# A causal mask added by matrix products instead of by VectorE and GpSimd, and a shorter routing chain, in a Perceiver-like layer

## The chip, the cores and the metric

The kernel runs on one core of a Trainium2 chip. The metric is the device time of one execution in microseconds; several executions are timed and the median counts. Engines are named as in the profile: PE (TensorE, the matrix engine), PEld (its weight loads), DVE (VectorE), ACT (ScalarE), POOL (GpSimd) and SP (SyncE, which here only issues DMAs).

## The reference

Two batches of 512 tokens of width 512 pass three blocks, each behind a layer norm and with a residual addition.

```python
x = x + cross_attention(norm(x), ctx, mask)   # 16 heads of 32, 8192 keys per batch
x = x + self_attention(norm(x))               # 16 heads of 32, causal, 512 keys
x = x + mixture(norm(x))                      # 16 experts, top 2, capacity 64 per batch

# self-attention: amplitudes and phases
q_amp = softplus(x @ Wq_amp.T); q_phi = pi * tanh(x @ Wq_phi.T)     # and so for k
q_amp = q_amp / sqrt(mean(q_amp**2) + eps)
scores = (q_amp cos(q_phi)) . (k_amp cos(k_phi)) + (q_amp sin(q_phi)) . (k_amp sin(k_phi))
scores = where(tril, scores / sqrt(32) * exp(log_scale), -inf)
out = softmax(scores) @ v @ Wo.T

# mixture: a token's place among those of its expert
g = softmax(x @ w_router); p, ei = top_k(g, 2)      # first choices of all tokens, then second ones
pos = cumsum(one_hot(ei)) - 1                       # tokens beyond the capacity are dropped
y = sum_k p_k * expert[ei_k](x)                     # (silu(x Wg) * (x Wf)) Wp
```

## The kernel before

The layer is one straight program; its order on each engine is the order in which it is written. Matrix products are float32 where nothing else is said, and the trace shows each as two passes over the moving columns.

**Cross-attention** (0 to about 2520 us) runs over 64 steps, 16 chunks of 1024 keys by 4 groups of 4 heads. Work of the self-attention of batch 0 (norm, phases, amplitudes) is filled into its last steps, and `sa_tables` makes the constants of the self-attention early in it, on POOL, DVE and ACT: `s_minus`, and `causal`, a 128x128 tile that holds 0 where the key is not later than the query and -2^100 elsewhere.

**Self-attention** (`self_attention`, to about 2834 us) works on groups of 4 heads, `g` from 0 to 3 for each batch. The four heads lie on four bands of 32 partitions, so that four products with 32 contraction rows run side by side on PE, each into a PSUM bank of its own. All banks come from one ring of eight (`bank()`); a product waits until the bank's last reader is done. Scores are made twice:

- `score_max` makes them with queries on the partitions, in three parts per group (`x` 0: queries 384 to 511 against 512 keys; 1: 256 to 383 against 384; 2: the two others, against 256 and 128). DVE adds `causal` to the square on the diagonal (L1181, L1188) and takes each row's maximum, `scm` (L1182, L1189, L1190). `split` then cuts the maxima into three bfloat16 parts, and `max_rows` turns them into `rows` with 16 small bfloat16 products (L194) and a copy on ACT (L1207).
- `score_exp` makes them again with keys on the partitions (`product`, L1155), in three parts of key tiles 0, 1 and 2 with 3. A bfloat16 product with `s_minus` and `rows` subtracts the maxima (L1224, four row groups of 3 rows), ACT takes the exponential into `e` (L1227), and POOL sets the squares' upper part of `e` to zero by a selection over 4 heads at once (L1229):

```python
for own in ([e[:, :, 0:P]] if x < 2 else [e[:, :, 0:P], e[:, :, 2 * P : 3 * P]]):
    nc.gpsimd.affine_select(out=own, in_=own, pattern=[[0, 4], [1, P]],
        compare_op=ALU.is_ge, fill=0.0, base=0, channel_multiplier=-1)
```

`attend` writes the order: per group the three exponentials, between them the maxima of four parts further on (`AHEAD`), then the weighted values (L1242) and the row sums (L1283) of two key tiles, `max_rows` of the next group, and the other two tiles. A chain on DVE ends the group (transpose, reciprocal, transpose, product: `srec`, `few`, `wide`, `soT`, L1303 to L1308) and frees the two banks of values and sums. `first_maxima` makes the first four parts of the maxima ahead of `attend`, between other products. In gaps named by group and part (`fill`) stands work of the other batch: for batch 0 the amplitudes and values of batch 1, for batch 1 the routing of batch 0.

**Routing** (`route`, once per batch) returns a list of pieces: norm statistics of four token tiles, `scale` (root and one Newton step), the four tiles normalised and stored to the DRAM tensor `normed`, four turns on PE into `mxnT`, then `router` (16 products, L764, and the row maximum, the differences and their exponential), `probabilities`, `top(0)` and `top(1)` (one-hot of first and second choice, `oh`), `counted` (running sums over the tiles on DVE, `so_far`), `ranked` (three products, L806, L809, L810, give each token's place; `hit` and `whose`) and `numbered` (16 PE instructions, L835, give each expert's list of tokens, `token`). For batch 0 the pieces lie in the gaps of batch 1's attention. For batch 1 they run after it, in a plain line: four times the output projection of a tile (`output`, L194, then L1316 on DVE) with its statistics and one expert's loads on SP, then all other pieces. Then POOL issues 16 gathers (`fetch`, `gx`, L852), which wait for `token` and the stores, and the **experts** start (L873, L890) and end at about 2963 us. The results are gathered back and added.

Of the kernel before, what the change touches and what calls it, by code (L numbers as in the profile page):

```python
# [20 lines left out]
P = 128  # L21
# [21 lines left out]
def perceiver_kernel(ctx: ExitStack, tc: tile.TileContext, a, out: bass.AP):  # L43
# [45 lines left out]
    lnp = ctx.enter_context(tc.tile_pool(name="ln", bufs=2))  # L89

    def norm_pieces(b, keep=None, aside=False):
# [52 lines left out]
        tiles = Tiles()  # L144
        pieces = [lambda i=i: stats(i) for i in range(TB)]
# [584 lines left out]
    def route(b, ps, pstag, ps1):  # L730
# [24 lines left out]
        pr, mx, sr = tile("pr", [P, TB, E]), tile("mx", [P, TB]), tile("sr", [P, TB])  # L755
        oh = tile("oh", [P, 2, TB, E])
        pk[b] = tile("pk", [P, 2, TB])

        def router():
            bank = ps1.tile([P, TB, P], F32, tag="j", name="pl")  # L760
            pl = bank[:, :, :E]
            for i in range(TB):
                for c in range(ND):
                    nc.tensor.matmul(  # L764
                        pl[:, i, :],
                        mxnT[:, c, i * P : (i + 1) * P],
                        mo.wr[:, c, :],
                        start=(c == 0),
                        stop=(c == ND - 1),
                    )  # L770
            nc.vector.tensor_reduce(mx, pl, AX.X, ALU.max)
            nc.vector.tensor_tensor(pr, pl, over_e(mx), ALU.subtract)
            nc.scalar.activation(pr, pr, AF.Exp)

        def probabilities():
            nc.vector.tensor_reduce(sr, pr, AX.X, ALU.add)
            nc.vector.reciprocal(sr, sr)
            nc.vector.tensor_tensor(pr, pr, over_e(sr), ALU.mult)

        def top(k):  # L780

            nc.vector.tensor_reduce(pk[b][:, k, :], pr, AX.X, ALU.max)
            eq, fm = tile(f"eq_{k}", [P, TB, E]), tile(f"fm_{k}", [P, TB])
            nc.vector.tensor_tensor(eq, pr, over_e(pk[b][:, k, :]), ALU.is_equal)
            nc.vector.tensor_tensor(eq, eq, over_t(mo.falling), ALU.mult)
            nc.vector.tensor_reduce(fm, eq, AX.X, ALU.max)
            nc.vector.tensor_tensor(oh[:, k], eq, over_e(fm), ALU.is_equal)
            if k == 0:
                nc.vector.scalar_tensor_tensor(pr, oh[:, k], -4.0, pr, ALU.mult, ALU.add)


        so_far = tile("sofar", [P, 2, TB, E])

        def counted():
            nc.vector.tensor_copy(so_far[:, :, 0, :], oh[:, :, 0, :])
            for i in range(1, TB):
                nc.vector.tensor_tensor(so_far[:, :, i, :], so_far[:, :, i - 1, :], oh[:, :, i, :], ALU.add)
# [3 lines left out]

        def ranked():

            bank = ps1.tile([P, S], F32, tag="j", name="pp")
            pp = bank[:, : 2 * TB * E].rearrange("p (k t e) -> p k t e", k=2, t=TB)
            nc.tensor.matmul(  # L806
                bank[:, : 2 * TB * E], mo.before, oh.rearrange("p k t e -> p (k t e)"), start=True, stop=False
            )
            nc.tensor.matmul(pp[:, :, 1:, :], ones, so_far[:, :, : TB - 1, :], start=False, stop=False)  # L809
            nc.tensor.matmul(  # L810
                pp[:, 1], ones, so_far[:, 0, TB - 1 : TB, :].to_broadcast([P, TB, E]), start=False, stop=True
            )
            for k in range(2):
                t, f = tile(f"rank_{k}", [P, TB, E]), tile(f"from_{k}", [P, TB, E])
                nc.vector.tensor_tensor(f, oh[:, k], over_t(mo.first_slot), ALU.mult)
# [676 lines left out]
```

## Time and profile before

| | before |
|---|---|
| median of 3 executions | 3010.15 us |
| lowest and highest | 3001.26 and 3014.18 us |
| the profiled execution | 3000.01 us, span 2998.3 us |
| mean granted clock of PE | 0.988 |
| busy share of PE, DVE, ACT, POOL | 97%, 67%, 47%, 73% |

The profile is of one execution. Its span runs from the first to the last instruction, and some 1.7 us lie around it. A line of the profile's groups reads: line of the kernel, engine, operation, what it writes and reads, shapes, count; then busy time and mean duration of one in ns; then the idle time of the engine just before and what ended it. PE's products are pipelined: the duration of one includes its way through the array, so what a product costs in a row is read from the starts. PE is busy for most of the span, so a step on another engine counts only where PE waits for it, and a step on PE counts nearly always.

### The profile page before, as it was taken

The page shows a single profiled execution, that of the slowest core. Times are in us where ns is not written, and L with a number is a line of the kernel's source. Part 1 is how long each engine was busy: PE and PEld are TensorE (multiplying, and loading weights), DVE is VectorE, ACT ScalarE, POOL GpSimd, SP SyncE. Part 2 cuts the span into 40 slices and gives each one's busy share as a digit, 9 for nine tenths or more (in the row PEclk, how much of TensorE's full clock was granted, in tenths as well). Part 3 has the DMA queues.
Part 4 walks back from the last instruction along what each step waited for, and adds up shares of the span by engine and source line. Part 5 has one row for each costly group of instructions (what it writes and reads, how often), then busy time and mean ns, then how long its engine had stood idle before and what let it go on. Part 6 is the DMA issues. An engine that isn't in the chain of part 4 may idle for free.

```text
span 2998.3 us, 64624 instructions
## 1 busy us (share of the span) xinstructions
PE 2899.7 (97%) x27911; PEld 1112.5 (37%) x27911; DVE 1997.8 (67%) x3397; ACT 1394.9 (47%) x2609; POOL 2175.4 (73%) x873
## 2 busy tenths in 40 slices
PE   7999999999999999999999999999999999999875
PEld 2333333333333333333333333333333332344564
DVE  6566777777777777766777776677777666668522
ACT  1355555555555555445555555555555436563210
POOL 1598888888888888978888888888888772011022
PEclk9999999999999999999999999999999999999987
DMA  3000000000000000000000000000000002011384
GB/s 124 1 24 1 24 2 24 2 24 6 20 8 18 16 9 23 2 1 24 1 24 2 24 1 24 1 24 1 24 2 1 29 30 71 1 43 45 105 259 128
DMA packets 48141, 89.65 MB, mean 30 GB/s; under 512 B 4720, under 2 KB 23152, under 8 KB 47856
## 3 DMA queue, kind: packets, MB, share of 16 engines
q1 hardware_dynamic: 40832, 70.31, 7.1%
q0 software_dynamic: 2752, 8.39, 0.9%
q10 hardware_dynamic: 4272, 6.83, 0.7%
q8 instruction: 218, 3.57, 0.5%
q14 instruction: 67, 0.55, 0.1%
HBM read 77.13 MB, written 8.39 MB: 29 GB/s over the span
## 4 chain that ended last, share of the span: by engine, by line
PE 92%; DVE 4%; ACT 1%; issue 1%; DMA 1%; POOL 1%; ACTq 0%; POOLq 0%; DVEq 0%
PE s L194 31%; PE s L423 18%; PE s L488 16%; PE s L436 15%; PE s L455 4%; PE s L1155 2%; PE ph L873 2%; PE s L515 2%; PE po L890 1%; DVE cm L445 1%; PE s L1242 1%; DVE acc L523 1%; PE s L1283 1%; PE s L167 0%; POOL r L918 0%
## 5 line engine op out<-in xcount | busy, mean ns | idle before, releaser
L654 POOL TENSOR_TENSOR es<-es,e 128x2048 f32<-128x2048 f32 x374 | 1700.7, 4547 | 54.9 <-ACT e L457 38.0
L457 ACT ACTIVATE e<-s 128x512 f32<-128x512 f32 x2048 | 1057.3, 603 | 1110.9 <-PE s L455 1110.9
L445 DVE TENSOR_REDUCE cm<-s 128x1 f32<-128x512 f32 x2048 | 1271.1, 683 | 330.8 <-PE s L423 330.7
L423 PE MATMUL s<-k,qT 32*128 32x512 f32 x4096 | 587.2, 640 | 3.4 <-DVE cm L445 1.9
L436 PE MATMUL s<-qT,k 32*128 32x512 f32 x4096 | 554.7, 593 | 3.1 <-ACT e L457 2.3
L488 PE MATMUL s<-e,v 128*32 128x512 f32 x4096 | 495.2, 600 | 1.1 <-DVE cm L445 0.8
L654 POOL TENSOR_TENSOR es<-e 128x2048 f32<-128x2048 f32 x63 | 286.2, 4542 | 243.0 <-ACT e L457 243.0
L194 PE MATMUL s<-wkv,ctx 128*32 128x512 f32 x3072 | 365.4, 596 | 0.4
L194 PE MATMUL s<-ctx,wkv 128*32 128x512 f32 x3072 | 355.9, 596 | 0.5
L436 PEld LDWEIGHTS s<-qT,k 32*128 32x128 f32 x4096 | 282.3, 184 | 185.1 <-issue 106.4
L503 DVE TENSOR_TENSOR acc<-acc,s 128x512 f32<-128x512 f32 (+1 forms) x359 | 207.8, 604 | 138.5 <-PE s L488 137.9
L423 PEld LDWEIGHTS s<-k,qT 32*128 32x128 f32 x4096 | 161.6, 182 | 330.7 <-issue 258.2
L488 PEld LDWEIGHTS s<-e,v 128*32 128x32 f32 x4096 | 107.4, 109 | 320.0 <-DVE cm L445 160.9
L455 PE MATMUL s<-rows,mb 4*128 4x512 bf16 x2048 | 218.0, 376 | 0.0
L399 DVE SCALAR_TENSOR_TENSOR k<-s,kf,m 128x512 f32<-128x512 f32 x128 | 96.1, 751 | 171.7 <-PE s L194 171.7
L194 PEld LDWEIGHTS s<-ctx,wkv 128*32 128x32 f32 x3072 | 87.1, 109 | 235.2 <-issue 154.3
L194 PEld LDWEIGHTS s<-wkv,ctx 128*32 128x32 f32 x3072 | 86.9, 109 | 214.3 <-issue 125.9
L414 ACT COPY v<-s 128x512 f32<-128x512 f32 x128 | 74.9, 585 | 98.1 <-PE s L194 77.3
L511 DVE TENSOR_TENSOR acc<-acc,s 128x1024 f32<-128x1024 f32 x56 | 68.4, 1221 | 71.1 <-ACT s L510 71.1
L455 PEld LDWEIGHTS <-mb 4*128 4x128 bf16 x2048 | 68.5, 93 | 105.5 <-issue 99.4
L1197 POOL TENSOR_TENSOR rest<-scm,parts 128x16 f32<-128x16 f32 x8 | 2.0, 254 | 139.9 <-DVE parts L1195 139.9
L1229 POOL TENSOR_SCALAR_AFFINE_SELECT e<-e 128x512 f32<-128x512 f32 x32 | 22.1, 703 | 105.9 <-ACT e L1227 105.9
(259 smaller groups left out, 1917.3 us busy)
## 6 DMA issues: line engine op xcount, KB each, us to landing
ctx<-in_ctxT_dram SPq DMA_DIRECT2D x45, 512.0 KB
wg<-in_L_ffn_w_gate_dram SPq DMA_DIRECT2D x16, 512.0 KB
wf<-in_L_ffn_w_fc_dram SPq DMA_DIRECT2D x16, 512.0 KB
wp<-in_L_ffn_w_proj_dram SPq DMA_DIRECT2D x16, 512.0 KB
results<-res ACTq DMA_DIRECT2D x32, 128.0 KB
m<-in_mask_BxS_bf_dram SPq DMA_DIRECT2D x16, 128.0 KB
w_wq_phiT<-in_wq_phiT_dram SPq DMA_DIRECT2D x2, 1024.0 KB
w_wq_ampT<-in_wq_ampT_dram SPq DMA_DIRECT2D x2, 1024.0 KB
```

The source lines that it names most:

```text
L194: nc.tensor.matmul(out[q], lhsT[:, q], rhs, start=start, stop=stop)
L399: nc.vector.scalar_tensor_tensor(k[:, keys], bank, kf[:, g, b : b + 1], mask_tiles[i][:, keys], ALU.subtract, ALU.mult)
L414: nc.scalar.copy(v[:, kt % (NKT // 2), :], bank)
L423: nc.tensor.matmul(s, qT(chunks[i][0], g, r, slice(qt * P, (qt + 1) * P)), k_tiles[n][r, hf * S : (hf + 1) * S], start=True, stop=True,)
L436: nc.tensor.matmul(s, k_tiles[n][r, keys], qT(chunks[i][0], g, r, slice(0, S)), start=True, stop=False)
L445: nc.vector.tensor_reduce(cms[g][chunks[i][1] % 2][:, qt, j : j + 1, hf], ss[j], AX.X, ALU.max)
L455: nc.tensor.matmul(ss[j], bias_tiles[i][r4, keys], rows[r4, :], start=False, stop=True)
L457: nc.scalar.activation(e[:, j, :], ss[j], AF.Exp)
L488: nc.tensor.matmul(av[j * HD : (j + 1) * HD, :], v_tiles[i][kt // (NKT // 2)][:, kt % (NKT // 2), h * HD : (h + 1) * HD], e[:, j, :], star ...
L503: nc.vector.tensor_tensor(dst, dst, src, ALU.add)
L511: nc.vector.tensor_tensor(acc[g], acc[g], pa.unsqueeze(1).to_broadcast([P, 2, S]), ALU.mult)
L654: nc.gpsimd.tensor_tensor(es, first if kt == 1 else es, e, ALU.add)
```

## The change

Two things are changed.

The **mask** of both kinds of scores becomes part of the scores' accumulation in PSUM. `sa_tables` no longer makes `causal`, but two bfloat16 tables on POOL: `which`, four stacked 32x32 unit matrices in the middle of zeros, and `bounds`, which holds 0, a triangle, and -2^100. A window of `which` as weights moves 32 rows of the mask to one quarter of the 128 output rows, so four products per head, 16 per square, add the whole mask. Additions on DVE and selections on POOL go.

The **routing** finds the first choice from the differences to the maximum (equal to 0) before the exponential is there, counts with products alone (24 PE instructions for 6, no running sums on DVE), makes `hit` in two halves, and moves the probabilities behind `numbered`. For batch 1 `route` returns `in_line`: the first three tiles are normalised (on ACT) under the last output product and turned ahead of the fourth; the last turn's copy is shared by ACT and DVE; and a one-element sigmoid follows the routing.

```diff
-                        nc.vector.tensor_tensor(s[:, qt * P : w], s[:, qt * P : w], sa.causal, ALU.add)
+                    masked(ss, slice(qt * P, w), sa.later)          # score_max, x < 2
...
+                    masked(ss, slice(P, 2 * P), sa.later)           # score_max, x == 2, two squares
+                    masked(ss, slice(2 * P, 3 * P), sa.later)
...
                     product(ss, b, g, 1, slice(kt * P, (kt + 1) * P), 0, slice(kt * P, S), at)
+                    masked(ss, slice(w, w + P), sa.sooner, False)   # score_exp, every key tile
...
-                for own in ([e[:, :, 0:P]] if x < 2 else [e[:, :, 0:P], e[:, :, 2 * P : 3 * P]]):
-                    nc.gpsimd.affine_select(...)
...
+            def masked(ss, at, mask, last=True):
+                for n in range(4):
+                    for j in range(4):
+                        r, c = slice(j * HD, (j + 1) * HD), slice((3 - n) * HD, (7 - n) * HD)
+                        nc.tensor.matmul(ss[j][:, at], sa.which[r, c], mask[r, c], start=False, stop=(last and n == 3))
...
+        def top_first():
+            nc.vector.tensor_reduce(mx[:, 0], pl, AX.X, ALU.max)
+            nc.vector.tensor_tensor(d, pl, over_e(mx[:, 0]), ALU.subtract)
+            nc.scalar.activation(pr, d, AF.Exp)
+            nc.vector.scalar_tensor_tensor(eq, d, 0.0, over_t(mo.falling), ALU.is_equal, ALU.mult)
+            first(0, eq)                       # two more steps on DVE: oh[:, 0]
...
+        def counted(k):
+            nc.tensor.matmul(pp[:, k], mo.before, oh[:, k], start=(k == 0), stop=False)
+            for i in range(1, TB):
+                nc.tensor.matmul(pp[:, k, i:], ones, oh[:, k, : TB - i], start=False, stop=(i == TB - 1))
+            if k == 0:
+                for i in range(TB):
+                    nc.tensor.matmul(pp[:, 1], ones, oh[:, 0, i : i + 1, :].to_broadcast([P, TB, E]), ...)
...
-        return pieces + [router, probabilities, lambda: top(0), lambda: top(1), counted, ranked, numbered]
+        found = [top_first, lambda: (counted(0), top_second()), lambda: counted(1), ranked, numbered, probabilities]
+        def in_line(output, between):
+            last = TB - 1
+            for i in range(TB):
+                output(i)
+                tiles.stats(i)
+                between(i)                     # loads of an expert
+                if i == last - 1:
+                    tiles.scale_of(0, last)
+                    for j in range(last):
+                        tiles.scaled(j)        # normalised on ACT
+                        stored(j)
+            turn(ps, pstag, tiles[0], mxnT[:, :, :P], nc.scalar.copy)
+            tiles.scale_of(last, TB)
+            for j in range(1, last):
+                turned(j)
+            tiles.normed(last)
+            stored(last)
+            turn(ps, pstag, tiles[last], mxnT[:, :, last * P :], halves)   # ACT and DVE, half each
+            router()
+            for f in found:
+                f()
+            nc.scalar.activation(tile("warm", [P, 1]), eps, AF.Sigmoid)
+        return in_line if split else pieces + [router, *found]
```

The pieces of batch 0 keep their number and their gaps; what stands in the last three gaps is now `top_first` with `counted(0)` and `top_second`, then `counted(1)` with `ranked`, then `numbered` with `probabilities`.

## The prediction

> **What bounds the kernel now.** I read the page's busy shares first, then the stages of the second half as windows, then what PE waited for in the self-attention, then groups and single starts there, and last the chain at the end.
>
> ```profile
> PE 2899.7 (97%) x27911; PEld 1112.5 (37%) x27911; DVE 1997.8 (67%) x3397; ACT 1394.9 (47%) x2609; POOL 2175.4 (73%) x873
> ```
>
> PE is the bound as a whole. The 73% of POOL belong to the cross-attention, which the change doesn't touch. The stages that it does touch (columns: stretch, its length, then busy us and count for PE, PEld, DVE, ACT, POOL, then clock, DMA share, GB/s):
>
> ```profile
> 2606.00:2711.00 105.00, 98.59 (x1152) 41.25 (x1148) 72.08 (x145) 59.57 (x97) 15.54 (x33) 1.00 0.11 37
> 2711.00:2737.00 26.00, 26.00 (x289) 10.97 (x287) 21.79 (x48) 6.19 (x7) 1.85 (x4) 1.00 0.25 82
> 2737.00:2822.00 85.00, 77.85 (x870) 45.53 (x863) 55.85 (x150) 30.66 (x61) 16.93 (x27) 0.96 0.21 69
> 2834.00:2860.50 26.50, 10.71 (x70) 10.30 (x70) 11.59 (x46) 3.99 (x7) 3.28 (x4) 0.62 0.41 138
> ```
>
> In the self-attention (the first three) PE is idle for 6.4, 0 and 7.2 us only; DVE and POOL have slack. The last stretch is the routing of the second batch: PE is mostly idle, and a serial chain runs. What the idle time of PE in 2606 to 2822 waited for (us, times, longest):
>
> ```profile
> PE s L1155 <- DVE soT L1308: 3.1, 4, 2.0
> PE s L1155 <- ACT e L1227: 3.0, 6, 0.6
> PE s L835 <- DVE whose L826: 2.3, 1, 2.3
> PE s L1155 <- DVE scm L1190: 1.4, 1, 1.4
> PE s L194 <- DVE scm L1190: 1.2, 1, 1.2
> PE s L1155 <- ACT rows L1207: 0.7, 1, 0.7
> PE s L194 <- DVE scm L1182: 0.7, 1, 0.7
> PE s L1155 <- DVE sr L776: 0.5, 1, 0.5
> PE s L194 <- DVE soT L1308: 0.5, 1, 0.5
> ```
>
> No line names POOL: the selections on GpSimd are never what PE waits for. Only 3.3 us (1.4, 1.2, 0.7) are the reductions of the maxima, behind the additions of `causal`.
>
> **The change, part by part.**
>
> *Products of the mask, on the path.* `masked` is called 4 times per group of heads in the maxima and 4 times in the exponentials: 64 calls for 8 groups, each 16 bfloat16 products of 32 rows, 128 columns of weights, 128 moving columns: four sets of four that run side by side, one per row group. The built program shows them, 1024 in all, each with its own weight load. The nearest thing in the trace is the subtraction of the maxima on a 128-wide tile, L1224, also bfloat16 in four row groups:
>
> ```profile
> 2634.48 0.40 PE L1155 MATMUL s<-sn 32*128 32x128 f32 x8
> 2634.59 0.12 PEld L1224 LDWEIGHTS <-s_minus 3*128 3x128 bf16 x4
> 2634.70 0.24 PE L1224 MATMUL s<-rows,s_minus 3*128 3x128 bf16 x4
> 2634.70 0.31 PEld L1155 LDWEIGHTS s<-phi 32*128 32x128 f32 x6
> 2634.76 0.66 PE L1155 MATMUL s<-phi 32*128 32x512 f32 x3
> ```
>
> Read the starts, not the durations, which include the drain: the set starts at 2634.70 and the next product at 2634.76. A set costs 0.06 us, and the 128 columns of weights for the next product, loaded from 2634.70 into the same row groups, hide in it. So a call costs 4 x 0.06 = 0.24 us and 64 calls 15.4 us. Lower bound: the 16 bfloat16 products of `max_rows` start at 2641.38 and the next product at 2641.60, 0.22 us per call, 14.1 us. Upper bound: a pass of four float32 products of 128 columns, 0.40 us shown for two passes and 0.11 between starts (2634.48, 2634.59): 64 x 4 x 0.11 = 28.2 us. I take 0.06, the row of the same type and form.
>
> [...]
>
> *Additions of `causal`, removed.* 64 of 291 ns and 32 of 425 ns: 32.2 us of DVE. Of this only the 3.3 us of waits for `scm` lie on PE. I count all 3.3 as gone. The waits for `soT` (3.6 us, five places) and for `rows` (0.7) end with chains that keep their length (transpose, reciprocal, transpose, product: 0.72, 0.25, 0.71, 0.69), but a product of maxima or exponentials with its mask stands in PE's order between the start of that chain and the wait, so each of the six is shortened by one call, 6 x 0.24 = 1.4. Together -4.7 us; bounds 0 and -7.6 (all three kinds gone). The waits for ACT's exponentials stay: the mask lies before the exponential.
>
> *Selections on GpSimd, removed.* 32 of 703 ns, 22.1 us, and nothing off the path. The product that reads `e` now waits for ACT alone. The weight loads waited 2.9 us for POOL, but PE was busy with row sums meanwhile. Bounds 0 and -2.9; I take 0.
>
> ```profile
> L1229 POOL TENSOR_SCALAR_AFFINE_SELECT e<-e 128x512 f32<-128x512 f32 x32 | 22.1, 703 | 105.9 <-ACT e L1227 105.9
> L1181 DVE TENSOR_TENSOR s<-s,causal 128x128 f32<-128x128 f32 x64 | 18.6, 291 | 9.4 <-PE s L1155 9.4
> L1188 DVE TENSOR_TENSOR s<-s,causal 128x256 f32<-128x256 f32 x32 | 13.6, 425 | 11.2 <-PE s L1155 11.2
> ```
>
> *Tables at the start.* POOL makes `which` and `bounds` (thirteen operations, at most 0.3 us each by the select of 128x128, 0.29) in place of two. POOL's next work after 19.8 us is at 71.8 us, `running_max`: nothing, and up to 3.4 us if that cover were missing.
>
> *Routing of the first batch, inside its second attention.* Before: 6 PE instructions in 0.9 us and waits of 2.3 and 0.5. Now 24 PE instructions at 0.117 (router, 3.75 us for 32), 2.8 us, in two gaps. `counted(0)` waits for the first one-hot, behind it on PE stands the next exponential: group 2's chain ends about 2805.9, five DVE steps of 0.257 end 2807.2, PE is there at 2805.4, so 1.8 us of wait. That wait swallows the later ones (0.7 and 0.5 us before the next score products), and `numbered` now stands a whole exponential and the products of two key tiles behind `ranked`, so its 2.3 are gone. 2.8 + 1.8 against 0.9 + 2.3 + 0.5 + 0.7: 4.6 against 4.4. Taken as 0, bounds -2 and +2.
>
> *Routing of the second batch, the chain at the end.* The last output product ends at 2833.89 in both.
>
> ```profile
> 2841.01 3.91 PE s L764 x32
> 2844.94 0.24 DVE mx L771
> 2849.41 0.77 PE s L806 x2
> 2853.47 1.87 PE s L835 x16
> ```
>
> Three tiles are now normalised and turned ahead of the last: statistics (0.70, 0.70, 0.19), root and five small steps (1.2) and 0.56 bring the fourth to 2837.75, one turn and a split copy to the router at 2838.7, 3.9 us later 2842.6, not 2844.9: -2.3. Then five steps instead of eleven to the first one-hot (1.3 for 2.8): -1.5. The second takes six as before. Counting: 16 products' instructions start under the second one-hot, 8 after it; at 0.117 the ranks come 1.6 us after it, where they came 1.86 after: -0.3. At the granted clock of 0.5 that the chain has from 2844 to 2864 I price them by the turns (3.27 / 16 = 0.204): 3.6 after, +1.8. The numbering starts after one half of `hit`, 1.05 us after the ranks and not 2.2: -1.15. Sum -5.2 to -3.1; I take -4. The probabilities moved behind the numbering run under the gathers of `gx` (4.14 us). The stores of `normed` and the loads keep their order on SP; the gathers, alone on POOL, start 4 us earlier.
>
> *First experts.* PE idled 6.4 us as "issue" from 2869.9 to 2878, with DMA share 0.89, ACT and DVE held as well. The change moves it, no row tells its size after; a sigmoid table load (1.28) is brought forward. I take 0, bounds -6.4 and +3.
>
> **Sum.** 15.4 - 4.7 + 0 - 4 = +6.7 us. The profiled execution took 3000.0 us (span 2998.3), 10.1 below the median of 3010.15; on it 3006.7, on the median 3016.8: **3017**, +0.2%. About 0.5%, 15 us, is what a measurement of this kernel can tell from no change.
>
> **Rivals.** *Sets that don't hide their loads (slower).* Four sets in a row into one row group and one bank: at 0.11 a set, 28.2 - 4.7 - 4 = +19.5, 3030. It decides from a set price of 0.093 us (23.8 us of masks). For it: only single sets are shown. Against: float32 sets of 128 columns follow at 0.11, which is their streaming time alone. *DVE relief is worth more (faster).* All 7.6 us of waits go, the tail gives 5.2, the stall at the experts 6.4, and the two stretches of 3.4 us at half clock after 2762 (some 3.4 us lost) don't come back: 14.1 - 7.6 - 5.2 - 6.4 - 3.4 = -8.5, 3002; over 0.5% only with the other bounds (-2.9, -2) as well, -13.4, and a little more. *The change doesn't reach what it names:* if the router's half clock and the wait of `counted(0)` eat the shorter chain, the tail gives 0 and batch one +2: +12.7, 3023.
>
> **Numbers.** Forecast 0.36, the last rival 0.12, the slower one 0.34 (the one sure term is PE's added 14 us; the gains are waits), the faster one 0.18, of which 0.11 go beyond 0.5%. So faster 0.11, within 0.5% 0.36 + 0.12 + 0.07 = 0.55, slower 0.34. The range takes the faster rival's 3002 and a little, and the slower one's 3030 and a little: 3000 to 3034.
>
> **What would show it.** The new line with `bounds,which`: starts 0.06 apart per set and about 15 us in all; at 0.11 the slower rival is right. No `scm` waits on PE, POOL nearly idle there. The first gather of `gx` about 4 us closer to the last output product. If the stage 2606 to 2822 is not 8 to 13 us longer, the absorbed waits were mis-sized.

## The result, and the profile after

The changed kernel is faster: **3002.29 us** in the median of 7 executions (2998.14 to 3003.65), the kernel before 3009.7 us beside it (7 executions, 3001.26 to 3014.18). The ratio is 0.9976, with a 95% interval of 0.9967 to 0.9986; a second series gave 0.9974 (0.9964 to 0.9984). That is 7.4 us, where 6.7 us more had been forecast. The profiled execution took 3002.29 us (span 3000.6); that of before, 3000.0, is near the fast end of its own times, so the two profiles are compared stage by stage and not by their ends.

The page's first line, then the stages that the prediction showed, 4.85 us later because the self-attention began so much later in this execution (columns as before):

```profile
PE 2918.0 (97%) x28971; PEld 1134.4 (38%) x28971; DVE 1957.8 (65%) x3292; ACT 1397.1 (47%) x2614; POOL 2156.2 (72%) x854
```

```profile
2610.85:2715.85 105.00, 103.53 (x1592) 48.05 (x1584) 56.72 (x105) 57.32 (x94) 3.62 (x17) 1.00 0.11 37
2715.85:2741.85 26.00, 26.00 (x364) 10.70 (x358) 14.61 (x30) 7.88 (x10) 0.75 (x3) 1.00 0.24 83
2741.85:2826.85 85.00, 80.84 (x1349) 54.23 (x1352) 43.05 (x114) 31.11 (x62) 9.41 (x11) 0.98 0.21 70
```

DVE and POOL are relieved as forecast (in the three stretches DVE has 114.4 us instead of 149.7, POOL 13.8 instead of 34.3). What PE waited for from 2600 to 2822 has shrunk to five lines; `scm` and `whose` are gone, and the wait of score products for `soT` comes once and not four times (us, times, longest):

```profile
PE s L1259 <- DVE soT L1410: 1.8, 1, 1.8
PE s L840 <- DVE oh L804: 1.5, 1, 1.5
PE s L1259 <- ACT e L1339: 1.1, 3, 0.4
PE s L1259 <- ACT rows L1318: 0.4, 1, 0.4
PE s L220 <- DVE soT L1410: 0.3, 1, 0.3
```

The mask products, as one line of the source, and one call among its neighbours in the timeline (start, busy, engine, line):

```profile
L1272 PE MATMUL s<-bounds,which x1024: 214/214/309, 2599.8 to 2819.0; 32*128 32x128 bf16 x171
```

```profile
2632.65 0.40 PE L1272 MATMUL s<-bounds,which 32*128 32x128 bf16 x16
2632.88 0.88 PE L1259 MATMUL s<-phi 32*128 32x384 f32 x8
```

From the start of the call at 2632.65 to the next product is 0.23 us. In 27 of the 64 calls it is 0.223 to 0.235 us; the others are longer, up to 1.7. At 0.223 us 64 calls are 14.3 us, and four sets in a row do hide their weight loads: the loads of L1272 take 93 ns each (median of 1024), and the sets follow at 56. Yet the self-attention, from the start of its first score product to that of its last output product, takes 240.2 us after (2598.02 to 2838.26) and took 240.1 before (2593.17 to 2833.25). 14.3 us went in, and it is no longer. The experiments ask what paid for them.

### The profile page after: what moved, and what is told of

Same layout as the page of the kernel before. It is cut to its first block, busy times and chain, and to the rows that moved or that the text cites. A ratio compares the mean times of both kernels' runs of the same rounds, so it can differ in the third digit from the quotient of the medians.

```text
span 3000.6 us, 66617 instructions
## 1 busy us (share of the span) xinstructions
PE 2918.0 (97%) x28971; PEld 1134.4 (38%) x28971; DVE 1957.8 (65%) x3292; ACT 1397.1 (47%) x2614; POOL 2156.2 (72%) x854
## 4 chain that ended last, share of the span: by engine, by line
PE 94%; DVE 3%; ACT 1%; issue 1%; DMA 1%; POOL 0%; ACTq 0%; POOLq 0%; DVEq 0%
PE s L220 31%; PE s L449 18%; PE s L514 16%; PE s L462 15%; PE s L481 4%; PE s L1259 2%; PE ph L953 2%; PE s L541 2%; PE po L970 1%; DVE cm L471 1%; PE s L1344 1%; PE s L1272 1%; DVE acc L549 1%; PE s L1385 1%; DVE acc L529 0%
## 5 line engine op out<-in xcount | busy, mean ns | idle before, releaser
L680 POOL TENSOR_TENSOR es<-e 128x2048 f32<-128x2048 f32 x63 | 286.1, 4541 | 242.9 <-ACT e L483 242.9
L998 POOL DMA_INDIRECT r<-results,get x16 | 16.3, 1020 | 97.0 <-DMA results<-res 92.5
```

Source lines behind the costliest of these rows:

```text
L680: nc.gpsimd.tensor_tensor(es, first if kt == 1 else es, e, ALU.add)
```

## The experiments

Theory 1: the additions and selections held single bands of PE, which the trace books as busy time; taking them away repaid the products. Theory 2: the prediction's sum is right for the mask, and the routing brought more than was thought. Theory 3: only the stretches in which PE runs at half clock moved. Each kernel was timed against the kernel before on its own chip; 0.1% is 3 us. The lengths are those of the self-attention in one profile. The two columns before them are explained below the table: the mean granted clock of PE, in thousandths above that of before on the same chip, and the microseconds against before that are left at equal clock.

| run | additions | selections | products | routing | ratio [95%] | clock | at equal clock, us | length, us | of it at half clock |
|---|---|---|---|---|---|---|---|---|---|
| before | yes | yes | no | old | 1 | 0 | 0 | 240.1 | 6.8 |
| before_again | yes | yes | no | old | 0.9993 [0.9983, 1.0003] | +0.8 | -0.3 ± 1.0 | 242.9 | 13.7 |
| mask_only | no | no | all | old | 0.9986 [0.9978, 0.9995] | +2.6 | +1.0 ± 1.1 | 240.2 | 3.4 |
| route_only | yes | yes | no | new | 0.9989 [0.9979, 0.9998] | +1.0 | -2.5 ± 1.0 | 240.5 | 10.2 |
| changed kernel | no | no | all | new | 0.9976 [0.9967, 0.9986] | not given | not given | 240.2 | 3.4 |
| after_again (the same) | no | no | all | new | 0.9974 [0.9964, 0.9984] | +3.6 | +0.3 ± 1.3 | 240.2 | 3.4 |
| no_mask | no | no | no | old | 0.9954 [0.9941, 0.9966] | +3.5 | -7.7 ± 1.5 | 229.9 | 0 |
| no_mask_again | no | no | no | old | 0.9960 [0.9946, 0.9973] | +2.7 | -7.3 ± 1.5 | 232.9 | 6.8 |
| no_add | no | yes | no | old | 0.9981 [0.9972, 0.9990] | 0.0 | -5.6 ± 1.0 | 236.7 | 13.7 |
| add_no_sel | yes | no | no | old | 0.9968 [0.9958, 0.9979] | +2.2 | -4.5 ± 1.3 | 236.0 | 6.8 |
| max_only | no | yes | maxima | old | 0.9988 [0.9979, 0.9997] | +0.5 | -2.0 ± 1.0 | 239.8 | 10.2 |
| mask_twice | no | no | all, twice | new | 1.0022 [1.0014, 1.0031] | +1.9 | +11.5 ± 1.0 | 251.1 | 3.4 |
| all_three | yes | yes | all | old | 1.0010 [1.0000, 1.0020] | +2.6 | +8.1 ± 1.1 | 249.2 | 10.2 |
| add_twice | twice | yes | no | old | 1.0068 [1.0055, 1.0081] | -2.8 | +13.0 ± 1.5 | 262.5 | 34.1 |
| route_no_add | no | yes | no | new | 0.9967 [0.9955, 0.9979] | +1.1 | -6.5 ± 1.3 | 234.4 | 10.2 |
| route_exp_mask | no | no | exponentials | new | 0.9990 [0.9980, 1.0000] | +0.8 | -2.1 ± 1.0 | 239.4 | 10.2 |
| chain_plain | no | no | all | new, tiles in the old order | 0.9995 [0.9986, 1.0005] | +2.0 | +2.3 ± 1.1 | 240.2 | 3.4 |
| best | no | yes | no | new, table early | 0.9953 [0.9939, 0.9966] | +3.5 | -6.2 ± 1.5 | 236.1 | 10.2 |

The half-clock time is that of the granted clock in the trace, where it comes in pieces of 3.4 us. Against the same step of another profile of the same kernel without it, one such piece lengthened a step by 1.3 and one by 1.7 us (no_mask_again, no_mask), but also one by 0.4 and one by 2.2 (before_again, before). The expectations below take half of it as what it cost.

The timed runs tell it better. Each reports its mean granted clock, to 0.001. Among executions of one kernel on one chip, 0.001 less goes with 2.1 us more (1.9 to 2.3 on each of the four chips; 256 executions, 1.5 us of scatter about the line). Since 0.001 of the span is 6 us at half clock, a microsecond at half clock goes with some 0.35 us of time. The column "at equal clock" is the difference of the mean times less 2.1 us for each 0.001 of clock, an estimate with its 95% interval. It matters here because before itself has a mean clock of 0.984 on two of the chips and of 0.986 and 0.987 on the others, so that ratios taken on different chips hold different amounts of it. (In the changed kernel's first series the clock of before is not given.) The profiles agree with it: with 0.35 of the half-clock time taken off, the lengths of the eight other kernels and series with the old routing differ from the mean of before's two, 237.9, by what that column says, within 0.5 us (add_twice 250.6, 12.7 longer; mask_only 239.0, 1.1 longer; no_mask 229.9, 8.0 shorter).

**The two parts apart.** mask_only: the kernel before with the mask products, without additions and selections, and with its old routing. route_only: the changed kernel with the old mask.

```diff
# mask_only: before.py plus
+ masked(...) four times per group in score_max, four times in score_exp
- additions of causal, affine_select of e
# route_only: after.py with these undone
```

> The kernel before with the mask products alone, its old routing kept. Theory 1, hidden waits: the 1024 products cost PE their 14.3 us, and additions and selections that are gone give as much back, more than the 4.7 us that PE's listed waits told, because PE counts as busy while one of its four bands waits: within 3 us of the kernel before, ratio 0.999 to 1.001. Theory 2, the sum of the prediction holds for the mask (+10 us) and the routing gives far more than its trace shows: 3016 to 3022 us, ratio 1.003. Theory 3, nothing but the phase of the clock gate differs between executions: same as the kernel before.

> The changed kernel with the old mask (additions on VectorE, selections on GpSimd), the new routing kept. Theory 1: the routing has all of the measured gain, 3 to 8 us faster than the kernel before, ratio 0.9975 to 0.999, the first gather 1 to 4 us nearer to the last output product. Theory 2: 15 to 18 us faster, ratio 0.994 to 0.995. Theory 3: same as before.

Measured: 0.9986 and 0.9989, some 4 and 3 us faster; together 0.9975, which is the changed kernel. Theory 2 falls: it wanted the mask 10 us slower and the routing some 15 faster. The mask alone is faster in time. At equal clock it is not: 1.0 us slower (-0.1 to 2.1), with 5.3 us that go with a clock 0.0026 higher, and the routing is 2.5 us faster there. The changed kernel's second series says the same: its mean is 7.1 us below before, its clock 0.0036 higher, which is 7.4 us, and 0.3 us (-1.0 to 1.6) is what is left. Its profile has one piece at half clock and a length of 240.2, as was expected of after_again below. So the gain goes with half clock, as theory 3 had it, though it stays from series to series, and at equal clock the products and the old mask work about cancel, as theory 1 had it.

**Neither old mask work nor products.** no_mask applies no mask at all.

```diff
- nc.vector.tensor_tensor(s[...], s[...], sa.causal, ALU.add)     # both places
- nc.gpsimd.affine_select(out=own, in_=own, ...)                  # of e
```

> The kernel before without the additions of causal and without the selections: no causal mask at all is applied, so its self-attention looks at all keys that it computes. It bounds what these two cost. Theory 1: some 14 us faster, ratio 0.995, because they cost as much as the products that replace them. Theory 2: only the 4.7 us of the listed waits, ratio 0.9984. Theory 3 as theory 2 or less.

> Edit: no_mask once more (no additions, no selections, no mask products, so no mask is applied; routing as before), for a second profile on another chip. If having no stretch at half clock in the self-attention belongs to this kernel, its profile has none or one, the length is 229.9 to 231.6, the spread of its times is about 1 us again, ratio 0.9954. If the first profile was chance, there are 2 to 4 stretches, 233 to 237 us, and a spread of 6 to 10 us.

Measured 0.9954 and 0.9960 (0.9946 to 0.9973): the additions and selections together cost 12 to 14 us, where the prediction had 4.7. At equal clock they cost 7.7 and 7.3; the rest goes with the clock. The second profile has 6.8 us at half clock, and the times spread by 6 us, so the absence of it in the first was chance.

**Control.** The kernel before once more.

```diff
(no edit)
```

> The kernel before itself, as a control of what two series of the same program differ by and for a second profile of it. All theories: ratio 1.000. Theory 3 expects a profile that is up to 10 us longer than the first one's 2998.3 us, with the difference in stretches at half clock outside the stages that the change touches; theories 1 and 2 expect the self-attention from its first score product to its last output product at 240 us again.

Measured 0.9993, an interval that holds 1. Its profile is 2.8 us longer in the self-attention than the first one, with 6.8 us more at half clock. So profiles of one kernel differ here by about what was to be explained, and only timed runs, and lengths corrected for that time, are read further. The control's own mean clock differs by 0.0008 from the other series of before, so differences in clock of that size say nothing.

**Additions and selections apart.** no_add takes the maxima over the whole score tile (an upper bound is enough, since the exponentials are masked later); add_no_sel keeps the additions, with a `causal` of zeros, and drops the selections, so it applies no mask.

```diff
# no_add
- nc.vector.tensor_tensor(s[...], s[...], sa.causal, ALU.add)
# add_no_sel
- nc.gpsimd.affine_select(out=sa.causal, ..., fill=-BIG, ...)
- nc.gpsimd.affine_select(out=own, in_=own, ...)
```

> Edit: the kernel before, without the additions of `causal` on VectorE; the maxima are then taken over the whole score tile, future keys included (any upper bound of the scores will do there), and the selections on GpSimd stay. Routing as before. 96 DVE instructions, 32.2 us of DVE, go; nothing is added on TensorE. The run without any mask work was 15.4 us below the kernel before; this one divides that sum between DVE and GpSimd. Theory 1 (what the additions held back was single bands of TensorE, which the trace shows as long busy products and not as idle time; the selections held nothing): 12 to 15 us faster, about 2995. Theory 2 (the selections on GpSimd held the products of e, and these the banks): 0 to 5 us faster, about 3006. Theory 3 (what counts is the number of stretches at half clock in the self-attention, each worth some 1.7 us; they follow waits of TensorE of about 2 us): the gain goes with the number of such stretches that are gone, at most 3 to 7 us.

> Edit: the kernel before with `causal` all zero (the additions run, but mask nothing), and without the selections on GpSimd: no mask is applied, every other step is as before. The fourth corner beside the kernel before (additions and selections), no_add (selections alone) and no_mask (neither). Measured so far: no_add 5.7 us below before, no_mask 13.8 us below by its ratio. In the traces the self-attention is 240.1 to 242.9 us long before, 236.7 in no_add, 229.9 in no_mask, of which 6.8, 13.7, 13.7 and 0 us ran at half clock; half of that taken off, the lengths are 236.5, 229.9, 229.9. Theory A (the additions cost some 6.5 us directly, the selections nothing directly, but they keep the stretches at half clock): 3 to 5 us faster than before (ratio 0.9983 to 0.999), length 236 to 238 with at most one such stretch. Theory B (the selections hold the path themselves): 8 to 10 us faster, ratio 0.997. Theory C (the selections matter only once the additions are gone): within 2 us of before.

Measured 0.9981 and 0.9968: 5.7 and 9.6 us, on different chips; at equal clock 5.6 and 4.5. Theory 1 had all of it in the additions, and is wrong there: the selections, which the prediction had at 0, cost about as much. Theory A of add_no_sel is refuted by the time. Theory B gives the time, but only about half of that is held directly, and the other 4.5 us go with a clock 0.0022 higher, which was theory A's idea. Of the 4.5 direct ones 2.2 are found in the trace.

The trace shows where the larger part sits: in the first group of the second batch. From the start of `soT` of the last group before it to the start of its own, one window each of before, no_add and the changed kernel:

```profile
2713.86:2760.81 46.95, 45.16 (x462) 20.20 (x458) 41.01 (x94) 12.03 (x20) 9.59 (x12) 1.00 0.08 28
```

```profile
2712.51:2755.51 43.00, 41.18 (x462) 20.06 (x458) 29.79 (x67) 12.03 (x20) 10.63 (x12) 1.00 0.09 31
```

```profile
2721.09:2766.11 45.02, 43.67 (x686) 23.75 (x677) 29.81 (x66) 13.23 (x21) 8.30 (x8) 1.00 0.07 25
```

All at full clock. Before, DVE is busy for 41.01 of 46.95 us, and with 11.2 us less of DVE the same 462 products take 3.95 us less. PE counts as busy for 45.16 us all the same. One line of before's timeline holds six of eight products, and 3.10 us, and the next band's weights wait for the reduction that frees their bank:

```profile
2748.21 3.10 PE L1155 MATMUL s<-phi 32*128 32x512 f32 x6
...
2748.63 0.29 PEld L1155 LDWEIGHTS s<-phi 32*128 32x128 f32 x2 [0.64 <-DVE scm L1190]
```

Reductions end at 2748.57, 2749.57 and 2750.56, and the next band's first product starts at 2748.63, 2749.62 and 2750.62; the line counts as busy throughout. The changed kernel's eight products at the same spot:

```profile
2755.58 0.66 PE L1259 MATMUL s<-phi 32*128 32x512 f32 x3
...
2755.75 1.07 PE L1259 MATMUL s<-phi 32*128 32x512 f32 x5
```

And within this stage lies half of the selections' part. `combine` multiplies cosine and sine by the amplitude at the same moment, one on DVE (`phi`), one on POOL (`sn`), both released by the same DVE operation. Before, POOL's line and DVE's:

```profile
2743.16 2.34 POOL L1148 TENSOR_TENSOR sn<-sn,amp 128x1024 f32<-128x1024 f32 x1 [1.20 <-DVE amp L1146]
```

```profile
2743.18 3.40 DVE L1147 TENSOR_TENSOR phi<-phi,amp 128x1024 f32<-128x1024 f32 x1
```

In add_no_sel, DVE's and POOL's:

```profile
2744.22 1.23 DVE L1138 TENSOR_TENSOR phi<-phi,amp 128x1024 f32<-128x1024 f32 x1
```

```profile
2744.25 3.40 POOL L1139 TENSOR_TENSOR sn<-sn,amp 128x1024 f32<-128x1024 f32 x1 [3.90 <-DVE amp L1137]
```

In the rows read here the one that starts 20 to 90 ns earlier takes 1.23 us on DVE or 2.34 on POOL, and the other takes 3.40 us (3.34 in no_add). Before, DVE loses: 3.40 instead of 1.23, 2.18 us, in the stage that DVE bounds. The step from `soT` to `soT` is 46.95 us before and 44.77 in add_no_sel: 2.18. In the five profiles with additions and selections (before, before_again, route_only, add_twice, all_three) DVE loses this start, in the thirteen others it wins. So it wins in no_add as well, and the same 2.18 us are part of no_add's 3.95: the two savings overlap. Why POOL is first where both are there is not shown, nor where the other 2.3 us of the selections sit. Either loser takes a little less than the two winners' times in a row (1.23 and 2.34, 3.57); what holds it is not shown.

**More for DVE.** Every addition twice.

```diff
  nc.vector.tensor_tensor(s[...], s[...], sa.causal, ALU.add)
+ nc.vector.tensor_tensor(s[...], s[...], sa.causal, ALU.add)
```

> Edit: the kernel before with each of the 96 additions of `causal` made twice, 32.2 us more on VectorE, nothing else changed. Theory A (DVE holds single banks of TensorE in the second batch, where it is busy 84% of a stretch): 7 to 15 us slower, more than the 5.7 that taking them away brought, ratio 1.0023 to 1.005. The prediction's account (DVE has slack, only 3.3 us of the additions lie on the path): 3 to 5 us slower, ratio 1.001 to 1.0017.

Measured 1.0068, 20 us slower (16 to 24): more than either expectation. At equal clock it is 13.0, within theory A's 7 to 15; the rest goes with a clock 0.0028 lower. In the profile:

```profile
2592.27:2854.78 262.51, 241.73 (x2536) 110.56 (x2534) 193.46 (x463) 109.22 (x178) 36.10 (x63) 0.93 0.14 45
```

34.1 us are at half clock. Of 32.2 us more of DVE 13 come through at equal clock, where the prediction's account had 3 to 5: DVE had much less slack than its 67% told, which is an average over stages.

**More for PE.** mask_twice issues every masked call twice; all_three adds the products to the kernel before and takes nothing away; max_only has them in the maxima alone.

```diff
# mask_twice
  masked(...)
+ masked(...)
# all_three: before.py plus masked(...) everywhere, additions of ident in place of causal
# max_only: before.py plus masked(...) in score_max, minus the additions; affine_select stays
```

> Edit: the changed kernel, with each of the 64 calls of masked products issued twice (the mask is added twice, the largest negative twice as large). 1024 more bfloat16 products, 14.3 us of TensorE at 0.223 us a call; DVE, ScalarE and GpSimd are the same. Theory 1 (the first 14.3 us were repaid by work that went from DVE and GpSimd, and the products themselves are fully on the path): 12 to 14 us slower than the changed kernel, 3 to 7 us above the kernel before, ratio about 1.002. A rival, that the products fill time in which TensorE would stand anyway (waits for the reductions, the exponentials): 0 to 6 us slower than the changed kernel, ratio at most 0.9995.

> Edit: the kernel before with the 64 calls of mask products added, and nothing taken away: the 96 additions stay (of `ident`, for want of room for `causal`; with the mask already in place a one on the diagonal only raises an upper bound of the scores), and so do the 32 selections. TensorE has 14.3 us more to do, DVE and GpSimd as much as before. It tells two causes apart: did the stretches at half clock go from the self-attention because TensorE has more to do, or because DVE and GpSimd have less? Theory A (DVE and GpSimd hold single bands; relief there is what paid): the products fill part of the time in which TensorE stands, 8 to 9 us of 14.3 stay, stretches at half clock stay at 2 to 4: 8 to 10 us slower than before, ratio 1.0027 to 1.0033. Theory B (a busier TensorE keeps its clock): at most one such stretch, 3 to 5 us of the 9 come back: ratio 1.001 to 1.002. The prediction's sum (products wholly on the path): 14 to 15 us slower, 1.0047 to 1.005.

> Edit: the kernel before, with the products of the mask in place of the additions of `causal` in the maxima alone (32 calls of 16 products, 7.1 us at 0.223 us a call); the exponentials keep their selection on GpSimd. Routing as before. Theory 1: 7.1 paid, 12 to 15 repaid by the additions: 5 to 8 us faster, about 3002, and so below the kernel with both kinds of products (ratio 0.9986). Theory 2 (the selections are what repaid): 7.1 paid, 0 to 5 repaid: 2 to 7 us slower. Theory 3: no more than 3 us either way.

mask_twice: 1.0022, on another chip than the changed kernel. At equal clock the second copy costs 11.2 us of 14.3 (11.5 against 0.3), and by the two profiles, both with 3.4 us at half clock, 10.9 (251.1 against 240.2). The rival, that the products fill time in which PE stands anyway, had 0 to 6.

all_three: 1.0010, only 3 us (0 to 6) in time for the first copy, but 8.1 at equal clock. Where DVE and POOL have no mask work the first copy costs 8.7 or 8.3 there (mask_only against the two runs without a mask). So the first copy costs 8 to 9 us of 14.3 in both cases, and the old mask work 7 to 8, with the products or without: at equal clock they add up. The times alone (by the ratios 8.7 us there, 0.9986 - 0.9957, and 3 here) look as if products and old mask work shared their waits; the difference goes with the clock, 0.0026 higher in all_three than in before. What of the 14.3 us doesn't show is mostly idle time of PE that the products fill: in the self-attention it falls from 11.7 us in no_mask to 7.4 in mask_only, and from 13.6 before to 9.0 in all_three. That is theory B, a busier PE keeps its clock: 5.3 us go with it, where it said 3 to 5 come back. In the one profile of all_three, from the fast end of its times, this does not show (three half-clock pieces, before two and four), and how it comes about is open.

max_only came out at 0.9988, against no_add's 0.9981 on the same chip: 7.1 us of products for some 2 us, 3.6 at equal clock. Theory 1 had said 5 to 8 us faster than before, and it is 4, or 2 at equal clock.

**The routing's tail.** chain_plain: the changed kernel, but with batch 1's tiles normalised and turned in the old order.

```diff
-            in_line = route(1, bank, "j", bank, split=True)
-            in_line(lambda i: output(1, i), lambda i: load(3 + i) if i < 3 else None)
+            pieces = route(1, bank, "j", bank)
+            ...                       # output, statistics, loads, then all other pieces, as before
```

> Edit: the changed kernel, but the second batch's tiles are normalised and turned in the order of the kernel before, piece by piece behind the outputs (all four statistics, then root and steps for the four together, then four turns, then the router); the shorter chain of one-hots, the counting and the numbering stay. It divides the tail. By the prediction's steps the early normalising is worth 2.3 us and the rest of the chain 0.8 to 2.9: this kernel would be 2 to 3 us slower than the changed one, ratio about 0.9985. By the traces (last output product to the first turn of gathered rows 27.3 us before, 26.1 after, and 26.3 with the new routing alone) the whole tail is worth 1 to 1.3 us: then it lies within 1.5 us of the changed kernel, ratio 0.9976 to 0.998.

Measured 0.9995 (0.9986 to 1.0005): by the ratios 5.7 us slower than the changed kernel, more than either expectation, but on another chip. At equal clock it is 2.0 us slower (2.3 against 0.3), which is what the prediction's steps gave. In its profile PE is at half clock from 3.5 us after the last output product, and so in mask_only; there the first gather starts 25.6 us after that product with the new chain and 26.2 with the old one. The chain without the early normalising is thus worth 0.6 us at the same clock; the early normalising brings the router 2.5 us forward (5.4 instead of 7.9 us after the last output product).

**Two versions that keep the new routing.** route_no_add: no products, no additions, maxima over the whole tile, selections in the exponentials. route_exp_mask: products in the exponentials alone.

```diff
# route_no_add: after.py
- masked(...) everywhere
+ nc.gpsimd.affine_select(out=own, in_=own, ...)      # of e, as before
# route_exp_mask: after.py
- masked(ss, ..., sa.later)                           # the three calls in score_max
```

> Edit: the changed kernel's routing with neither additions nor products of the mask: the maxima over the whole score tile, as upper bounds, and the selection on GpSimd in the exponentials as in the kernel before. If the parts add up (routing alone was 0.9989, 3 us): Theory 1: 15 to 18 us faster than the kernel before, about 2992, ratio 0.9945. Theory 2: 3 to 8 us faster. Theory 3: 3 to 10 us faster, with a narrow spread if no stretch at half clock is left in the self-attention.

> Edit: the changed kernel without the products of the mask in the maxima (these are taken over the whole score tile, as upper bounds); the products in the exponentials stay. No additions, no selections, half of the mask products (7.1 us of TensorE). Theory A: 229.9 plus some 4 us for half of the products, 234 in the self-attention, with the shorter routing 7 to 10 us below the kernel before (ratio 0.997 to 0.9977), close to the run with selections and no additions (0.9967). Theory B (selections cost 8 to 10 directly, the products in the exponentials 4 to 7): 9 to 13 us below, ratio 0.996 to 0.997, the fastest of all that compute the whole function.

route_no_add: 0.9967, 10 us faster than before (6.5 at equal clock), less than theory 1's 15 to 18. route_exp_mask: 0.9990, and no theory had that; with 7.1 us fewer products it should lie below the changed kernel, and by its ratio it lies above, the intervals overlapping at their edges. At equal clock it does lie below, -2.1 against +0.3, less far than expected. Its clock is only 0.0008 above that of before, the changed kernel's 0.0036; why is open.

**The best version, and a table load.** best is route_no_add with the table of Exp loaded under the router.

```diff
             turn(ps, pstag, tiles[last], mxnT[:, :, last * P :], halves)
+            nc.scalar.activation(tile("hot", [P, 1]), eps, AF.Exp)
             router()
```

> Edit: route_no_add (the changed kernel's routing; maxima over the whole score tile, no additions; selections on GpSimd) with one ScalarE activation of a single column with Exp, issued behind the last copy of the turned tile and ahead of the router. In the changed kernel ScalarE loads the table of Exp (1.28 us) only once the first differences exist, because the root of the normalising took its place, and the second one-hot waits 0.89 us for the exponentials. With the table loaded under the router (5 us in which ScalarE idles) that wait is gone from the chain of waits: the second one-hot ends 1.5 to 1.6 us after the first, not 2.4, and the first gather starts 0.8 to 0.9 us earlier against the last output product than in route_no_add at the same clock. Ratio 0.9964, not to be told from route_no_add's 0.9967.

> Edit: none, the changed kernel once more beside the others on this chip, for a second profile. If one stretch at half clock in the self-attention belongs to it, the profile shows 0 or 1, length about 240; ratio 0.9976 again, within 0.001.

best: 0.9953 (0.9939 to 0.9966), 14 us faster than before; the changed kernel on the same chip 0.9974 (0.9964 to 0.9984). It cannot be told from route_no_add (6.2 and 6.5 us faster at equal clock), but by its ratio it is the fastest of the versions that compute everything. The table load behaved in part as expected. Two DVE lines of the changed kernel, then of best:

```profile
2851.31 0.23 DVE L817 SCALAR_TENSOR_TENSOR d<-oh,pr 128x64 f32<-128x64 f32 x1 [0.89 <-ACT pr L811]
...
2855.88 0.29 DVE L858 TENSOR_TENSOR rank<-s,oh 128x128 f32<-128x128 f32 x1 [2.53 <-PE s L842]
```

```profile
2844.84 0.23 DVE L817 SCALAR_TENSOR_TENSOR d<-oh,pr 128x64 f32<-128x64 f32 x1
...
2850.19 0.29 DVE L858 TENSOR_TENSOR rank<-s,oh 128x128 f32<-128x128 f32 x1 [3.31 <-PE s L842]
```

The wait of 0.89 us for the exponentials is gone, and the wait for the counting products is 0.78 us longer. The 24 products, at some 0.2 us each, were the bound; the load (1.28 us, at 2849.72 in the changed kernel) lay beside them. The gather starts 1.1 us earlier than in route_no_add, all of it in the router, for which DVE waits 3.93 us and not 5.00.

## Why the prediction was wrong, point by point

**What bounds the kernel.** PE was read as idle for 6.4, 0 and 7.2 us, DVE and POOL as having slack. This is one root, the clock the other. The stretch of 26 us without idle time at which DVE had 21.79 us was the beginning of the DVE-bound stage, and what followed to 2760.8 was not looked at by itself.

**Price of the products: right.** 0.24 us a call forecast, 0.223 measured where nothing holds it; the slower rival's 0.11 us a set is refuted for sets of four row groups: the four sets are 0.056 us apart. **Their place on the path: wrong for the first copy.** 15.4 us were taken as exposed, but for 1.4 of waits that they shorten; 8 to 9 were, at equal clock. They fill 4.4 to 4.6 us of PE's idle time, and the rest may lie where PE stands and the profile has it busy, as in the 3.10 us above; that is not shown. Of the second copy 11 were exposed.

**"Together -4.7 us" for the additions: the step that failed**, with the **0 for the selections**. The two together cost 12 to 14 us in time and 7 to 8 at equal clock. Only the waits listed for PE were counted, and no line there named POOL; but POOL came in through DVE (3.40 us for 1.23), and DVE through single banks.

**The clock, at nothing: the larger failure.** The sum has no term for how much of the time PE runs at half clock, and 10.1 us between the profiled execution and the median were carried over as if the changed kernel had to lose them too. The profiled execution of before ran at 0.988. In the runs whose clock is given, before has 0.984 on chips of like times (3008.9 and 3008.4 us), the changed kernel 0.988, which goes with 7.4 us. That the clock is higher both with less mask work and with more work for PE is measured (0.0035 and 0.0027 above before in the two series of no_mask, 0.0026 in all_three); what in them does it is not shown.

**The stage.** "If the stage 2606 to 2822 is not 8 to 13 us longer, the absorbed waits were mis-sized": it is not longer, and they were.

**First batch's routing, 0: right.** The last three steps from `soT` to `soT` are 22.9, 21.8 and 16.6 us in route_only, 22.8, 21.4 and 16.7 before. The wait for the first one-hot was put at 1.8 us and is 1.5.

**The tail: -4 forecast, -1.4 measured** (first gather 23.05 us after the last output product before, 21.68 after). Router 2.2 earlier (2.3 said); first one-hot 1.5 sooner (1.5 said); numbering 1.1 sooner behind the ranks (1.15 said). Against that the router, from its first product's start to its last's, took 5.1 us, not 3.7, as half clock now begins 1.5 us after its start and not 3.1 (2845.24 after, 2843.90 before; +1.4, forecast only in the rival "does not reach what it names"); and from the first one-hot to the ranks, where the prediction kept 1.55 for the second one-hot and bounds of -0.3 and +1.8, it became 2.0 us longer: 24 products at 0.2 us set it. The upper bound was the right one, because that clock stays at half:

```profile
2845.20:2869.10 23.90, 15.84 (x81) 15.20 (x81) 6.98 (x28) 3.02 (x4) 7.03 (x8) 0.50 0.49 153
```

**The balance.** At equal clock: 8.7 for the products, -7.5 for the old mask work, 0 for the first routing and -1.4 for the tail are -0.2, where the sum had +6.7, and 0.3 ± 1.3 is measured. The clock goes with 7.4 us more. Products too dear by 7 us and gains too small by 3 were partly made up by a tail too good by 2.6.

The faster rival had the sign and part of the reason ("DVE relief is worth more"), and its 7.6 us for the old mask work is what is measured. That its total is 3002 us as well is luck: it has 14.1 for the products, 5.2 for the tail, and 6.4 for a stall at the experts that stayed (first turn of gathered rows to last product of the experts 103.1 us before, 104.0 after). It alone had a term for the half clock, 3.4 us, where 7.4 go with the clock.

## What to carry to other kernels

A busy share of PE near 100% (97% here) doesn't say that PE is the bound where four bands work side by side: cut the span at the end of each group and look for the stretch in which another engine is busy nearly throughout (here DVE, 41.01 of 46.95 us). Price what an edit adds by starts, and what it removes by taking it away alone. Where the granted clock differs between executions, compare kernels at equal clock before adding up parts: here effects that did not add up in time did so then, and the whole measured gain went with the clock. Before making mask work cheaper, ask which of it is needed: maxima that only shift an exponential need no mask, and leaving that out was worth 5.6 us at equal clock, the whole change about nothing.

## What the runs showed of the hardware that was not expected

- Of two elementwise products of 128x1024 float32, one on DVE and one on POOL, that started 20 to 90 ns apart, the later took 3.40 us (3.34 in no_add), on either engine; the earlier took 1.23 on DVE and 2.34 on POOL.
- PE's granted clock drops to 0.50 in pieces of 3.4 us inside a stage in which it is booked as busy for over 94% of the time (226.5 of 240.1 us before). Of the 43 such stretches in the 18 profiles 20 stand behind a wait of 1.5 to 2.3 us, the others behind waits of under 1 us or none. In the changed kernel, the piece after the 1.8 us wait for `soT`:

```profile
2766.70:2770.10 3.40, 3.15 (x18) 1.48 (x21) 2.42 (x6) 0.00 (x0) 0.00 (x0) 0.50 0.06 17
```

  The same wait, 2.0 us in no_mask, was followed by none. In each of the 18 profiles all half-clock stretches start whole multiples of 3.413 us apart; in the changed kernel's the first starts at 42.9 us and the one above 798 of these later, at 2766.7. That the same wait may count or not because of where it lies against this raster fits the traces, but was not tested.
- On two of the chips the first experts' stage was 9 us or more shorter for every kernel (94 us, not 103 to 105, from the first turn of gathered rows to the last expert's product): in 23 us from that turn the DMA engines moved 298 GB/s in no_add, 251 in before_again.
